# A graph layer that fetches source rows in three ways: gathers made to wait for ScalarE's copies, a new share for each way, and another order of the last octets

## The chip, the cores and the metric

One core of a Trainium2 chip runs the kernel. Its engines are TensorE (PE), VectorE (DVE), ScalarE (ACT), GpSimd (POOL) and SyncE (SP), each with an instruction stream of its own, and they wait for one another by semaphores. Times are microseconds (us) of device time for one execution. The profile is one execution seen by the hardware profiler: which engine did what, when, and what ended each wait. The clock that the profile lists is the share of full speed that TensorE was granted.

## The reference

A graph has 12,500 nodes with 64 features `x` and 400,000 edges, sorted by their destination `dst`; each edge has a source `src` and 16 attributes. One message-passing layer with a residual and a layer norm:

```
m_in = concat([x[src], x[dst], edge_attr], -1)
h = silu(m_in @ W1 + b1)
messages = silu(h @ W2 + b2)
agg = segment_sum(messages, dst, num_segments=12500)
y = silu(concat([x, agg], -1) @ W3 + b3)
out = layernorm(x + y, -1)
```

## The kernel before

**Tiles and octets.** 128 edges are a tile, and there are 3125 tiles. Eight tiles make an octet (`OT`), so that there are `NO` = 391 octets; the last has five tiles. Three octets make a chunk (`CT` = 24 tiles). The main loop runs over the octets by a counter `o`, which I call a turn, and its order on PE, ACT, DVE and SP is written out by hand (`tc.manual_schedule`); GpSimd's instructions go in the order in which they are issued.

**What an octet needs.** The first layer's input is summed in PSUM by TensorE (`first_layer`): the part of the source nodes, the part of the destination nodes (a window of `S` = 48 nodes, since `dst` is sorted) and the part of the attributes. ScalarE turns it into `h` (line 490). The second layer (`second_layer`) multiplies by W2, and ScalarE makes the messages `m` (line 505). `add_up` sums the messages of an octet by destination with one-hot matrices `eh`, and `add_window` (line 519, VectorE) adds the result at the window's place in `agg`. These steps belong to different turns: the second layer comes `SECOND` = 2 turns after the first, `add_up` `THIRD` = 4 and `add_window` `LAST` = 6, and the last few octets have shorter lags (`times`).

**Three ways to a source row.** The part of the source nodes comes

- by **gathers**: GpSimd issues an indirect DMA for each tile (`gather`, line 383), 128 rows of 64 numbers. In octets below `RAW` = 12 it reads `x`, from then on the table `pa` = x @ W1 (its first rows), which `table` builds in the first turns. The five buffers `ga` (`AHEAD` + 2) are filled three turns ahead; a buffer is free again when TensorE's first layer five octets earlier has read it.
- by **columns**: ScalarE and VectorE copy single columns of the transposed `x`, which lies in SBUF (`xs`), into a tile `cx` of 128 columns that holds two tiles of edges (`columns`, lines 307 and 309). The address of every column comes from a register; the registers are loaded from SBUF in groups (line 299). ScalarE makes `ACOLS` in two parts of 36, ahead of `h` and ahead of `m`; VectorE makes `VCOLS` in four parts, 68 in all. 256 copies replace two gathers of one octet; these octets are listed in `pairs`. The index list of each is loaded by SyncE (`index`) and turned into addresses by VectorE (`address`, line 368). Columns are made from octet `BEGIN` = 6 until `QUIET` = 6 octets ahead of the last.
- by **rows**: SyncE fetches single rows of `pa` by DMAs with a register as address (`rows`, line 336), `ROWS` = 16 a turn. 256 of them replace two gathers of one octet too; these octets are listed in `rpairs`.

An octet so has eight gathers, six, or four.

**Nodes.** Where all edges of a group of 512 nodes are done, the group's output follows (`node_load`, `node_product`, `node_silu`, `node_stats`, `divide`, `store`) in the turns set by `later`. The last two groups (`rest` and the one behind it) come after the loop.

**The check of dst.** Windows only work if every octet's destinations lie within 48 nodes and node groups aren't closed too early. `limits` computes this at the end on VectorE and `verdict` sums it over partitions with TensorE. If it fails, a second way (`general`) computes the layer again; with these inputs it does not run.

Of the kernel before, what the change touches and what calls it, by code (L numbers as in the profile page):

```python
# [9 lines left out]
F32 = mybir.dt.float32  # L10
# [10 lines left out]
P = 128  # L21
# [5 lines left out]
SCT = 240  # L27
AHEAD = 3
SECOND = 2
THIRD = 4  # L30
# [3 lines left out]
TABLES = 7  # L34
ACOLS = ((12, 12, 12), (12, 12, 12))
VCOLS = ((20,), (16,), (16,), (16,))
ROWS = 16
XADDR = 37088
QUIET = 6
LAG = CT * P // 32  # L40
# [62 lines left out]
def windows(ctx, tc, ident, identb, badi, pa, x, xt, xt2, src_c, src_row, dst_c, dst_row, attr_t, attr_2, base, w1, b1, w2, b2, w3, b3, out, edges):  # L103
# [154 lines left out]
    with tc.tile_pool(name="gat", bufs=AHEAD + 2) as gat, \  # L258
# [16 lines left out]
        while True:  # L275
# [3 lines left out]
            pairs.append(o)  # L279
        cols, indices = {}, {}  # L280
        xb = xs.bitcast(U8)

        def columns(o, eng, part):
# [5 lines left out]
            while cuts or left:  # L289
# [12 lines left out]
                for e, r in zip(range(e0, e0 + n), regs):  # L302
                    h = slice(e // P * D, (e // P + 1) * D)
                    to, frm = t[h, e % P * 4:e % P * 4 + 4], xb[:D, ds(r - XADDR, 4)]
                    if eng == ENG.DVE:

                        nc.vector.tensor_reduce(to, frm[:, :, None], AX.X, OP.max)  # L307
                    else:
                        nc.scalar.copy(to, frm)  # L309
                lo += n  # L310
# [11 lines left out]
        def rows(o):  # L322
            lo = (o - RAW) * ROWS
            j, e0 = lo // (2 * P), lo % (2 * P)
            if o < RAW or j >= len(rpairs):
                return
            if e0 == 0:
                single[rpairs[j]] = rx.tile([P, 2, D], F32, name="rx")
            t = single[rpairs[j]].bitcast(U8)
            if o % 2 == 0:  # L330
                _, rowreg[:] = nc.values_load_multi_w_load_instructions(
                    rindex[j][0:1, e0:e0 + 2 * ROWS], engines=(ENG.SP,), min_val=0, max_val=4 * D * (N - 1),
                    skip_runtime_bounds_check_because="src names a node")
            for e in range(e0, e0 + ROWS):
                r = rowreg.pop(0)
                nc.sync.dma_start(t[e % P:e % P + 1, e // P, :], pab[ds(r, 4 * D)].rearrange("(o n) -> o n", o=1))

        def rbegun(o):
            j = (o - RAW) * ROWS // (2 * P)
            return o >= RAW and (o - RAW) * ROWS % (2 * P) == 0 and j < len(rpairs), j  # L340

# [32 lines left out]
        def gather(o):  # L374
            c, t0, n, first, last = octs[o]
            ga = gat.tile([P, OT, D], F32, name="ga")
            sc = srcs[t0 // SCT][:, t0 % SCT:]
            if n % 2:
                nc.vector.memset(ga[:, n, :], 0.0)
            for i in range(n):  # L380
                if o in (pairs, rpairs)[i // 2 % 2] and i < 4:
                    continue
                nc.gpsimd.indirect_dma_start(  # L383
                    out=ga[:, i, :], out_offset=None, in_=x if o < RAW else pa[:, :],
                    in_offset=bass.IndirectOffsetOnAxis(ap=sc[:, i:i + 1], axis=0))
            got[o] = ga

# [215 lines left out]
        batches = [(q, min(q + RB, early - 1)) for q in range(0, early - 1, RB)]  # L603
        rest = early - 1
        for q in range(early):
            if q >= rest:
# [14 lines left out]
        def limits():  # L621
            evi = xs.bitcast(I32)[:, :3 * NCH]
            nc.gpsimd.iota(evi, pattern=[[STEP, NCH], [0, 3]], base=0, channel_multiplier=0)
            lag = xs[:, 3 * NCH:3 * NCH + NO]
            nc.vector.tensor_tensor(lag, evi[:, :NO], wb, op=OP.subtract)
            lim = nv.tile([P, 3], F32, name="lim")
# [22 lines left out]

        seconds = times({None: SECOND, 0: 1, 1: 1, 2: 1})  # L650
        adds = times({None: THIRD, 0: 2, 1: 2, 2: 2, 3: 3, 4: 3, 5: 3})
        folds = times({None: LAST, 0: 3, 1: 4, 2: 4, 3: 5})

        for o in range(min(AHEAD, NO)):
            gather(o)
# [14 lines left out]
        with tc.manual_schedule(engines={ENG.PE, ENG.Activation, ENG.DVE, ENG.SP}):  # L670
# [4 lines left out]
            for o in range(NO + 2):  # L675
# [31 lines left out]
                if o + 1 < NO - 1:  # L707
                    window_product(o + 1)
                if o % 4 == 0 and 4 <= o < NO + 4:
                    bases(ENG.DVE, o - 4)  # L710
                for q in folds.get(o, []):
# [27 lines left out]
                if 30 <= o < 30 + 2 * LP and o % 2 == 0:  # L739
                    k = (o - 30) // 2  # L740
                    part = rel[:, k * TILES // LP:(k + 1) * TILES // LP]
                    nc.vector.tensor_reduce(lims[:, 0, k:k + 1], part, AX.X, OP.min)
                    nc.vector.tensor_reduce(lims[:, 1, k:k + 1], part, AX.X, OP.max)
                if o >= 1:
                    for c in tables[(o - 1) * per:o * per]:
# [15 lines left out]
                if o == NO - 3:  # L761
                    node_product(rest, 1)
                if o == NO - 2:
                    for q in range(rest + 1, NG):
                        node_product(q, 1)


            for i in range(NO + 2, NO + LAST):
                for q in folds.get(i, []):
                    add_window(q)  # L770
            bad = limits()
            for q in behind.get(NO, []):
                node_silu(q)
            for f, a in todo.get(NO, []):
                f(*a)
            for q in range(rest, NG):
                node_product(q, 2)
                node_silu(q)
            for q in range(rest, NG):
                node_stats(q)  # L780
            verdict(bad)
            root(rest, NG)
# [261 lines left out]
```

## Time and profile before

| what | value |
|---|---|
| median of 3 runs | 5318.76 us (5303.48 to 5322.22) |
| the profiled execution | 5309.46 us |
| its span | 5307.7 us |
| mean granted TensorE clock | 0.644 |
| gathers, from `x` and from `pa` | 94 and 2575 |
| single rows fetched by SyncE | 5888 |
| column copies by ScalarE, by VectorE | 27000, 25480 |
| octets | 391 |

A group of the profile is read so: line, engine and operation, what it writes and reads, the count, busy time in all and the mean of one in ns, then the engine's idle time ahead of these instructions and what ended it. "issue" as the cause of idle time means that the engine waited for nothing that the profile can name. Copies overlap, so that 36 copies of 189 ns each take less than 36 times that. In a timeline the columns are start, length, engine, line, operation and count; in windows they are the stretch, its length, the busy time with the count in brackets, the granted clock, the share of DMA time and GB/s.

### The profile page before, as it was taken

The page shows a single profiled execution, that of the slowest core. Times are in us where ns is not written, and L with a number is a line of the kernel's source. Part 1 is how long each engine was busy: PE and PEld are TensorE (multiplying, and loading weights), DVE is VectorE, ACT ScalarE, POOL GpSimd, SP SyncE. Part 2 cuts the span into 40 slices and gives each one's busy share as a digit, 9 for nine tenths or more (in the row PEclk, how much of TensorE's full clock was granted, in tenths as well). Part 3 has the DMA queues.
Part 4 walks back from the last instruction along what each step waited for, and adds up shares of the span by engine and source line. Part 5 has one row for each costly group of instructions (what it writes and reads, how often), then busy time and mean ns, then how long its engine had stood idle before and what let it go on. Part 6 is the DMA issues. An engine that isn't in the chain of part 4 may idle for free. (4 is left out here: it accounts for less than half of the span.)

```text
span 5307.7 us, 110604 instructions
## 1 busy us (share of the span) xinstructions
PE 2676.8 (50%) x15336; PEld 1962.6 (37%) x15336; DVE 2676.6 (50%) x27690; ACT 3320.9 (63%) x27845; POOL 2520.4 (47%) x2678
## 2 busy tenths in 40 slices
PE   4644545444455455454554545544455455454555
PEld 3433333333333333333343333333333333333333
DVE  1555555545555555545555555555555555555552
ACT  1566666666666666666666666666666666666663
POOL 6444444444444444444444444444444444444443
PEclk6666666666666666666666666666666666666667
DMA  3111111111111111111111111111111111111111
GB/s 73 44 25 25 28 25 26 26 26 25 31 24 27 26 25 27 25 26 28 29 25 25 26 26 26 26 30 27 26 26 25 26 26 27 29 27 24 27 25 26
DMA packets 159906, 148.18 MB, mean 28 GB/s; under 512 B 103383, under 2 KB 111718, under 8 KB 158646
## 3 DMA queue, kind: packets, MB, share of 16 engines
q0 software_dynamic: 85408, 87.63, 8.7%
q1 hardware_dynamic: 59658, 45.35, 3.4%
q10 hardware_dynamic: 14092, 8.03, 0.6%
q14 instruction: 621, 5.09, 0.3%
q8 instruction: 127, 2.08, 0.2%
HBM read 134.37 MB, written 6.40 MB: 27 GB/s over the span
## 5 line engine op out<-in xcount | busy, mean ns | idle before, releaser
L309 ACT COPY cx<-xs 64x4 uint8 x27000 | 2879.8, 189 | 1568.0 <-issue 1534.5
L383 POOL DMA_INDIRECT ga<-pa,sc x2575 | 2429.3, 943 | 2679.8 <-PE p L483 1820.3
L307 DVE TENSOR_REDUCE cx<-xs 64x4 uint8 x25480 | 1946.1, 141 | 2076.7 <-issue 2045.6
L501 PEld LDWEIGHTS p<-w2d,h 128*128 128x128 f32 x3126 | 667.0, 315 | 2549.4 <-issue 2549.4
L499 PE MATMUL p<-b2r,one 3*128 3x512 bf16 x391 | 216.2, 553 | 2367.7 <-ACT m L505 1539.5
L501 PE MATMUL p<-w2d,h 128*128 128x128 f32 x3126 | 779.4, 427 | 3.0 <-issue 3.0
L487 PE MATMUL p<-oh,xw 128*128 128x512 f32 (+1 forms) x758 | 583.4, 865 | 0.9 <-issue 0.9
L514 PEld LDWEIGHTS pg<-eh,m 128*64 128x64 f32 x6250 | 248.5, 157 | 531.3 <-issue 266.5
L505 ACT ACTIVATE m<-p 128x512 f32<-128x512 f32 x391 | 231.8, 593 | 258.7 <-remote 164.7
L458 DVE COPY oh<-ph 96x512 f32<-96x512 f32 x391 | 266.1, 681 | 203.6 <-issue 193.0
L514 PE MATMUL pg<-eh,m 128*64 128x48 f32 x6250 | 299.4, 243 | 107.6 <-DVE agg L519 87.3
L483 PE MATMUL p<-ident,ga 128*128 128x128 f32 x1288 | 346.5, 411 | 1.3 <-issue 1.3
L490 ACT ACTIVATE h<-p 128x512 f32<-128x512 f32 x391 | 231.2, 591 | 76.7 <-remote 32.0
L483 PEld LDWEIGHTS p<-ident,ga 128*128 128x128 f32 x1288 | 276.1, 226 | 2.6 <-issue 2.6
L407 PE MATMUL mm<-w1bb,xr 65*96 65x128 f32 x782 | 265.5, 442 | 12.5 <-issue 5.4
L448 PE MATMUL ph<-identb,eh 128*96 128x128 bf16 x1563 | 245.2, 311 | 51.5 <-remote 21.6
L448 PEld LDWEIGHTS <-eh 128*96 128x96 bf16 x1563 | 233.0, 198 | 62.3 <-DVE oh L458 26.9
L430 DVE TENSOR_TENSOR eh<-wrow,dc 128x384 f32<-128x384 f32 x392 | 213.3, 544 | 10.5 <-remote 10.0
L487 PEld LDWEIGHTS p<-oh,xw 128*128 128x128 f32 x758 | 190.6, 308 | 0.9 <-issue 0.9
L407 PEld LDWEIGHTS mm<-w1bb,xr 65*96 65x96 f32 x782 | 170.7, 277 | 14.8 <-issue 10.0
L412 DVE TENSOR_TENSOR xw<-mm,mask 96x128 f32<-96x128 f32 x391 | 110.1, 281 | 125.4 <-issue 78.5
L486 PE MATMUL p<-cx,w1d 128*128 128x128 f32 x408 | 122.0, 399 | 0.0
(89 smaller groups left out, 945.5 us busy)
## 6 DMA issues: line engine op xcount, KB each, us to landing
rx<-pa SPq DMA_DIRECT2D x5888, 0.2 KB
ga<-pa,sc POOLq DMA_INDIRECT x2575
oh<-in_attr SPq DMA_DIRECT2D x130, 192.0 KB
xr<-in_xt SPq DMA_DIRECT2D x391, 24.0 KB
cxi<-in_src_row SPq DMA_DIRECT2D x205, 1.0 KB
xs<-in_xt ACTq DMA_DIRECT2D x6, 512.0 KB
pa<-v ACTq DMA_DIRECT2D x12, 256.0 KB
xa<-in_x SPq DMA_DIRECT2D x24, 128.0 KB
```

Of the source, the lines that this page charges most:

```text
L307: nc.vector.tensor_reduce(to, frm[:, :, None], AX.X, OP.max)
L309: nc.scalar.copy(to, frm)
L383: nc.gpsimd.indirect_dma_start(out=ga[:, i, :], out_offset=None, in_=x if o < RAW else pa[:, :], in_offset=bass.IndirectOffsetOnAxis(ap=sc ...
L407: nc.tensor.matmul(pw[:E, :], winrow[o], w1bb.rearrange("k s m -> k (s m)"), start=True, stop=True)
L448: nc.tensor.matmul(ph[:E, i, :], eh[:, i, :, 1], identb, start=(i == 0), stop=(i == k - 1), skip_group_check=True)
L458: nc.vector.tensor_copy(oh[:E, :], ph[:E, :(n + 1) // 2].rearrange("p i e -> p (i e)"))
L483: nc.tensor.matmul(p1[:, i, :], g2.rearrange("p s d -> p (s d)"), ident, is_transpose=True, start=(i == c), stop=False, skip_group_check=True)
L487: nc.tensor.matmul(p1[:, :k], xw[o % 3], oh, start=False, stop=True, skip_group_check=True)
L490: nc.scalar.activation(h[:, :k], p1[:, :k], AF.Silu)
L501: nc.tensor.matmul(p2[:, 2 * i:2 * i + 2, :].rearrange("p s d -> p (s d)"), h[:, i, :], w2d, start=False, stop=(i == k - 1), skip_group_ch ...
L505: nc.scalar.activation(m[:, :n2], p2[:, :n2], AF.Silu)
L514: nc.tensor.matmul(pg[s * D:(s + 1) * D, :], m[:, i, :], eh[:, i // 2, :, s], start=(i < 2), stop=(i >= n - 2), skip_group_check=True)
```

## The change

- **Waits.** Every column copy is noted in `steps` under the turn that makes it. A gather of octet `o` now also waits, by a dependency added by hand, for one of ScalarE's copies: with `LEAD` = 4 it is a copy of turn `o` - 4, and gather k of n waits for the copy that stands k/n of the way through that turn's list. Where there are no more copies than gathers there is no wait, as in the first turns.
- **Shares.** ScalarE makes 36 + 38 columns a turn instead of 36 + 36, VectorE 70 instead of 68, SyncE fetches 18 rows instead of 16. `rows`, `rbegun` and with them `rload` and `raddress` are written so that a list of 256 may begin within a turn. `QUIET` falls from 6 to 2.
- **The last octets.** The lags of the last eight octets are shortened: second layer 0 or 1 turns behind the first, `add_up` 1 or 2, `add_window` 2 or 3.
- **The last node groups.** Of the two groups behind the loop, the first is multiplied, put through silu and its statistics taken in the last two turns of the loop; only the last group stays behind it.
- **The check.** `limits` is cut in two. Its iota is issued ahead of the first gather and has 131 numbers instead of 393; the rest, `check`, runs in turn 51 (31 + 2 `LP`), `verdict` in turn 52.
- **Bases.** VectorE loads the window bases of four octets in turns 2, 6, 10 and so on, for octets from `o` - 2, instead of in turns 4, 8, 12 for octets from `o` - 4.

```diff
+LEAD = 4
+TURNS = (ENG.Activation,)
...
-ACOLS = ((12, 12, 12), (12, 12, 12))
-VCOLS = ((20,), (16,), (16,), (16,))
-ROWS = 16
+ACOLS = ((12, 12, 12), (12, 12, 14))
+VCOLS = ((20,), (16,), (18,), (16,))
+ROWS = 18
 XADDR = 37088
-QUIET = 6
+QUIET = 2
...
+        steps = {ENG.Activation: {}, ENG.DVE: {}}
...
-                        nc.vector.tensor_reduce(to, frm[:, :, None], AX.X, OP.max)
+                        done = nc.vector.tensor_reduce(to, frm[:, :, None], AX.X, OP.max)
                     else:
-                        nc.scalar.copy(to, frm)
+                        done = nc.scalar.copy(to, frm)
+                    steps[eng].setdefault(o - (eng == ENG.Activation and part == 0), []).append(done.ins)
...
         def rows(o):
-            lo = (o - RAW) * ROWS
-            j, e0 = lo // (2 * P), lo % (2 * P)
-            if o < RAW or j >= len(rpairs):
-                return
-            if e0 == 0:
-                single[rpairs[j]] = rx.tile([P, 2, D], F32, name="rx")
-            t = single[rpairs[j]].bitcast(U8)
-            if o % 2 == 0:
-                _, rowreg[:] = nc.values_load_multi_w_load_instructions(
-                    rindex[j][0:1, e0:e0 + 2 * ROWS], engines=(ENG.SP,), min_val=0, max_val=4 * D * (N - 1),
-                    skip_runtime_bounds_check_because="src names a node")
-            for e in range(e0, e0 + ROWS):
+            for lo in range((o - RAW) * ROWS, (o + 1 - RAW) * ROWS) if o >= RAW else ():
+                j, e = lo // (2 * P), lo % (2 * P)
+                if j >= len(rpairs):
+                    return
+                if e == 0:
+                    single[rpairs[j]] = rx.tile([P, 2, D], F32, name="rx")
+                if e % 32 == 0:
+                    _, rowreg[:] = nc.values_load_multi_w_load_instructions(
+                        rindex[j][0:1, e:e + 32], engines=(ENG.SP,), min_val=0, max_val=4 * D * (N - 1),
+                        skip_runtime_bounds_check_because="src names a node")
+                t = single[rpairs[j]].bitcast(U8)
                 r = rowreg.pop(0)
                 nc.sync.dma_start(t[e % P:e % P + 1, e // P, :], pab[ds(r, 4 * D)].rearrange("(o n) -> o n", o=1))
 
         def rbegun(o):
-            j = (o - RAW) * ROWS // (2 * P)
-            return o >= RAW and (o - RAW) * ROWS % (2 * P) == 0 and j < len(rpairs), j
+            j = -(-(o - RAW) * ROWS // (2 * P))
+            return o >= RAW and j * 2 * P < (o + 1 - RAW) * ROWS and j < len(rpairs), j
 
...
-            for i in range(n):
-                if o in (pairs, rpairs)[i // 2 % 2] and i < 4:
-                    continue
-                nc.gpsimd.indirect_dma_start(
+            todo = [i for i in range(n) if o not in (pairs, rpairs)[i // 2 % 2] or i >= 4]
+            for k, i in enumerate(todo):
+                g = nc.gpsimd.indirect_dma_start(
                     out=ga[:, i, :], out_offset=None, in_=x if o < RAW else pa[:, :],
                     in_offset=bass.IndirectOffsetOnAxis(ap=sc[:, i:i + 1], axis=0))
+                eng = TURNS[k % len(TURNS)]
+                ahead = steps[eng].get(o - LEAD - (eng == ENG.Activation), [])
+                if len(ahead) > len(todo):
+                    tc.add_manual_dep(g.ins, ahead[k * len(ahead) // len(todo)].name,
+                                      mybir.DependencyInfo(mybir.DependencyClass.Sync, mybir.DependencyReason.DATA))
...
         def limits():
-            evi = xs.bitcast(I32)[:, :3 * NCH]
-            nc.gpsimd.iota(evi, pattern=[[STEP, NCH], [0, 3]], base=0, channel_multiplier=0)
-            lag = xs[:, 3 * NCH:3 * NCH + NO]
-            nc.vector.tensor_tensor(lag, evi[:, :NO], wb, op=OP.subtract)
+            evi = nv.tile([P, NCH], I32, name="evi")
+            nc.gpsimd.iota(evi, pattern=[[STEP, NCH]], base=0, channel_multiplier=0)
+            return evi
+
+        def check(evi):
+            lag = nv.tile([P, NO], F32, name="lag")
+            f, k = NO // 3, NO // 3 * 3
+            nc.vector.tensor_tensor(lag[:, :k].rearrange("p (c t) -> p c t", t=3), evi[:, :f, None].to_broadcast([P, f, 3]),
+                                    wb[:, :k].rearrange("p (c t) -> p c t", t=3), op=OP.subtract)
+            if k < NO:
+                nc.vector.tensor_tensor(lag[:, k:], evi[:, f:f + 1].to_broadcast([P, NO - k]), wb[:, k:], op=OP.subtract)
...
-        seconds = times({None: SECOND, 0: 1, 1: 1, 2: 1})
-        adds = times({None: THIRD, 0: 2, 1: 2, 2: 2, 3: 3, 4: 3, 5: 3})
-        folds = times({None: LAST, 0: 3, 1: 4, 2: 4, 3: 5})
-
+        seconds = times({None: SECOND, 0: 0, 1: 0, **{k: 1 for k in range(2, 8)}})
+        adds = times({None: THIRD, 0: 1, 1: 1, **{k: 2 for k in range(2, 8)}})
+        folds = times({None: LAST, 0: 2, 1: 2, **{k: 3 for k in range(2, 8)}})
+
+        evi = limits()
...
-                if o % 4 == 0 and 4 <= o < NO + 4:
-                    bases(ENG.DVE, o - 4)
+                if o % 4 == 2 and o - 2 < NO:
+                    bases(ENG.DVE, o - 2)
...
+                if o == 31 + 2 * LP:
+                    bad = check(evi)
+                if o == 32 + 2 * LP:
+                    verdict(bad)
...
-                    node_product(rest, 1)
+                    node_product(rest + 1, 1)
                 if o == NO - 2:
-                    for q in range(rest + 1, NG):
-                        node_product(q, 1)
+                    node_product(rest)
+                    node_silu(rest)
+                if o == NO - 1:
+                    node_stats(rest)
 
 
             for i in range(NO + 2, NO + LAST):
                 for q in folds.get(i, []):
                     add_window(q)
-            bad = limits()
             for q in behind.get(NO, []):
                 node_silu(q)
             for f, a in todo.get(NO, []):
                 f(*a)
-            for q in range(rest, NG):
-                node_product(q, 2)
-                node_silu(q)
-            for q in range(rest, NG):
-                node_stats(q)
-            verdict(bad)
+            node_product(rest + 1, 2)
+            node_silu(rest + 1)
+            node_stats(rest + 1)
```

## What I expected

> **What bounds the kernel now.** I read the page first: busy times, then the costliest groups.
>
> ```profile
> PE 2676.8 (50%) x15336; PEld 1962.6 (37%) x15336; DVE 2676.6 (50%) x27690; ACT 3320.9 (63%) x27845; POOL 2520.4 (47%) x2678
> ...
> L309 ACT COPY cx<-xs 64x4 uint8 x27000 | 2879.8, 189 | 1568.0 <-issue 1534.5
> L383 POOL DMA_INDIRECT ga<-pa,sc x2575 | 2429.3, 943 | 2679.8 <-PE p L483 1820.3
> L307 DVE TENSOR_REDUCE cx<-xs 64x4 uint8 x25480 | 1946.1, 141 | 2076.7 <-issue 2045.6
> ```
>
> No engine is full. ScalarE is the fullest, and its 1568.0 us of idle time ahead of the column copies are nearly all "issue": it waited for nothing that the profile names. VectorE shows the same ahead of its own column copies. The waits by engine tell how such idle time is cut up:
>
> ```profile
> DVE cx L307 <- issue: 2045.6, 3031, 6.2
> ACT cx L309 <- issue: 1534.5, 2161, 5.5
> ```
>
> ScalarE has 2161 gaps of 1534.5/2161 = 0.71 us, VectorE 3031 of 0.67 us. GpSimd's idle time ahead of gathers is put down to TensorE's first layer (1820.3 us above): it issues an octet's gathers in one run and then waits for a buffer. To see whether the two belong together I read the timeline of two neighbouring octets, GpSimd and then ScalarE:
>
> ```profile
> 2022.08 0.94 POOL L383 DMA_INDIRECT ga<-pa,sc  x1 [8.85 <-PE p L483]
> ...
> 2030.82 0.94 POOL L383 DMA_INDIRECT ga<-pa,sc  x1 [0.30 <-issue]
> 2034.05 0.94 POOL L383 DMA_INDIRECT ga<-pa,sc  x1 [2.28 <-PE p L487]
> ...
> 2040.28 0.94 POOL L383 DMA_INDIRECT ga<-pa,sc  x1 [0.30 <-issue]
> ```
>
> ```profile
> 2016.82 0.60 ACT L505 ACTIVATE m<-p 128x512 f32<-128x512 f32 x1
> 2017.31 3.62 ACT L309 COPY cx<-xs 64x4 uint8 x36
> 2020.96 0.60 ACT L490 ACTIVATE h<-p 128x512 f32<-128x512 f32 x1
> 2021.45 3.52 ACT L309 COPY cx<-xs 64x4 uint8 x36
> 2024.88 0.58 ACT L505 ACTIVATE m<-p 128x512 f32<-128x512 f32 x1
> ...
> 2044.22 0.60 ACT L505 ACTIVATE m<-p 128x512 f32<-128x512 f32 x1
> ```
>
> One run has eight gathers, (2030.82 - 2022.08)/7 = 1.25 us apart, the next six. From one m to the next, ScalarE needs 8.06 us for the first octet (72 copies at 3.52/36 = 0.098 us, h and m) and 19.34 us for the second, which has the same work. Their mean, 13.70, is the kernel's mean octet, 5307.7/391 = 13.57. The same stretch in windows, with line 309's copies alone (length, busy time, count, clock):
>
> ```profile
> 2017.30:2021.00 3.70, 3.61 (x36) 0.50 0.00 1
> 2022.08:2025.85 3.77, 3.24 (x34) 0.95 0.14 29
> 2025.87:2033.36 7.49, 1.85 (x12) 0.56 0.13 27
> 2033.36:2037.38 4.02, 3.43 (x34) 0.82 0.25 65
> 2037.38:2042.57 5.19, 1.25 (x8) 0.50 0.17 31
> 2042.57:2048.40 5.83, 5.17 (x52) 0.50 0.01 2
> ```
>
> This is what bounds the kernel. For the first 3.3 to 3.8 us of a run of gathers ScalarE copies as fast as without any; then it makes 12 copies in 7.49 us and 8 in 5.19, and is fast again at 2033.36 and 2042.57. The slow stretch ends 11.28 us after the first of eight gathers (2022.08) and 8.52 after the first of six (2034.05), so at 1.38n + 0.24: it behaves like a backlog worked off at 1.38 us a gather, while GpSimd adds one every 1.25. After a pause of 2034.05 - 2033.36 = 0.7 us the next run had its full fast start again. The clock column doesn't go with it (0.56 and 0.50 slow, 0.50 and 0.95 fast).
>
> The Trainium skill speaks against all this: "SBUF — State Buffer", section "Who interferes with whom", says that DMA never contends with a compute engine and that "PE and ACT never wait on anyone". By it, moving gathers would give ScalarE nothing. The windows disagree (36 copies in 3.70 us against 12 in 7.49, one engine and line); what the rule would make of the time is the second rival.
>
> **The change part by part.**
>
> *The waits.* Gather k of n of octet X now waits for copy 74k/n that ScalarE makes in loop turn X-4. The old wait for the buffer (first layer of X-5) is met by then, as h of X-5 stands ahead of those copies. Behind a waiting gather stand only later gathers; TensorE waits for them in turn X, three turns after the last release, at least 24 us at 8.06 a turn. So lateness is covered; without that cover a 1.25 us gather would delay the first layer one for one. Released by copies 0, 12, 24, 37, 49, 61 (n = 6) the gathers form groups of three, cut by h and m; with n = 8, groups of four. 12 copies take 1.2 us and 9 take 0.9, both under 1.25, so within a group GpSimd sets the pace; but a slow ScalarE, at about 0.63 us a copy (7.49/12, 5.19/8), releases the next only after 5 to 8 us, so a run cannot grow through a slow stretch as it does now.
>
> A run of n costs the slow stretch less its copies: 12 x 0.098 of 7.49 and 8 x 0.098 of 5.19, so 85% of 1.38n + 0.24 - b, where b, the start, is 3.3 to 3.8. With b = 3.3 that is 6.8 us for eight, 4.4 for six, 2.1 for four, 0.9 for three. From octet 12 to 386 the loops give 160, 203 and 12 octets of eight, six and four gathers before, and 156, 201 and 18 after. Before: (160 x 6.8 + 203 x 4.4 + 12 x 2.1)/375 = 5.4 us an octet, and 8.06 + 5.4 = 13.5, near the 13.57 above. After, in two groups each: (156 x 4.2 + 201 x 1.8)/375 = 2.7. Saved: 2.7 at b = 3.3; with b = 3.8, 4.9 - 1.9 = 3.0. Runs of three and four are drawn down from the rows of six and eight. The bounds: groups of three may not reach the slow stretch at all, or groups may join across h, which lasts 0.6 us. I take off 0.1 for the second.
>
> *74, 70 and 18.* ScalarE: 2 x 0.098 = 0.2 us an octet, on the path. VectorE's two cost its group's (1946.1 + 2045.6)/25480 = 0.157 us each at most, 0.3, under ScalarE's 8.26; were that cover gone, they would add 0.3. SyncE's row transfers have a row of their own:
>
> ```profile
> 2016.89 2.46 SPq L336 DMA_DIRECT2D rx<-pa  x8
> ```
>
> 2 x 2.46/8 = 0.6 us more; 18 rows are 5.5 us, also within the octet. There are 213 column pairs for 205 and 26 row pairs for 23, hence 22 gathers fewer (2647), already in the counts above.
>
> ```profile
> L368 DVE TENSOR_SCALAR cxi<-cxi 1x256 int32<-1x256 int32 x205 | 56.2, 274 | 1.1
> ```
>
> Their index lists are eleven more (those of the rows cost about the same): 11 x 0.274 = 3 us of VectorE, under ScalarE; uncovered, 3 us.
>
> *The end.* Columns now reach the last octets, and gathers stay paced there. Before, a long run stands there:
>
> ```profile
> 5232.92 0.98 POOL L383 DMA_INDIRECT ga<-pa,sc  x1 [0.86 <-PE pg L514]
> ...
> 5251.68 0.94 POOL L383 DMA_INDIRECT ga<-pa,sc  x1 [0.30 <-issue]
> ...
> 5253.76 0.82 PEld L514 LDWEIGHTS pg<-eh,m 128*64 128x64 f32 x13 [9.79 <-issue]
> ...
> 5291.58 0.56 DVE L625 TENSOR_TENSOR xs<-xs,wb 128x391 f32<-128x391 int32 x1
> 5291.71 3.17 PE L554 MATMUL mm<-w3s,agg 128*128 128x64 f32 x16 [0.53 <-DVE agg L519]
> ```
>
> Sixteen gathers in a row, in which even TensorE stands 9.79 us. Cutting that run is worth about 10; the second last node group taken out of the final chain saves half of the 3.17 us of matmuls and its statistics, about 3; shorter lags 2. I take 15 in all, between 0 and 30. *The check of dst* leaves the end, where its first 0.56 us operation and those after it overlap the 3.17 us of matmuls, so that is worth nothing; in octet 51 it costs VectorE under 2 us once. The iota goes ahead of the first gather, which waits for its indices anyhow (below), and is a third as large:
>
> ```profile
> 2.84 1.11 POOL L383 DMA_INDIRECT ga<-in_x,sc  x1 [1.35 <-DMA sc<-in_src_c]
> ...
> 5230.83 1.23 POOL L623 IOTA xs<- 128x393 int32 x1
> ```
>
> The bases for VectorE are loaded two turns sooner, as many as before: nothing, or one register load of an octet if they hold up the queue.
>
> *The sum.* Per octet 2.8 (the middle of 2.7 and 3.0) - 0.1 - 0.2 = 2.5 us; 375 x 2.5 = 940; with the end 955. The profiled execution took 5309.5 us, 1.8 more than its span and 9 less than the median of the runs, which is within their spread. 5309.5 - 955 = 4350, rounded. For this case alone the gain lies between 1.8 and 3.3 us an octet: 4060 to 4620.
>
> **The rivals.**
>
> *No slow stretch is left.* Each wait may stretch GpSimd's step past 1.38 us, and the backlog never forms. Then 6.74 gathers an octet x 1.38 = 9.3 us bind, more than ScalarE's 8.26: 5309.5 - 375 x 4.3 - 15 = 3680. For it: in neither run did the first 3.3 us slow anything. Against: 1.2 us between releases, and POOL's step of 1.25.
>
> *ScalarE's gaps are its own.* If the slow copies have nothing to do with gathers, a copy costs (2879.8 + 1534.5)/27000 = 0.163 us, and 213 x 256 x 74/144 = 28,021 copies are 1021 more: +167, less 15 for the end, 5460. This is what the skill's rule in that section would give. Against it stand the six windows.
>
> *Every gather drags its own slow 1.38 us once they are spread (the slower side).* If the fast start of a run does not come back between spaced gathers, 6.74 x 1.38 x 0.85 = 7.9 us an octet are lost instead of 5.4: 375 x (2.5 + 0.2) more, 6320. It decides from the point where the mean gather costs more than 5.4/6.79 = 0.8 us. Against it: 0.7 us of pause brought the fast start back; for it: pauses inside a group will be shorter.
>
> *Runs of eight stay.* 8 x 1.25 = 10 us exceed an octet of 8.26, so GpSimd may fall behind and go on without waits. Octets of eight would keep 6.8: (156 x 6.8 + 201 x 1.8)/375 = 3.8, a gain of 1.4 an octet: 4770.
>
> **How the numbers follow.** Forecast 0.60, no slow stretch 0.16, runs of eight 0.11, gaps of its own 0.06, every gather 0.05, a gain under 0.5% for reasons not seen 0.02 (half a per cent is about what this measurement tells from none). Faster 0.87, same 0.02, slower 0.11. The range, 3650 to 4900, takes in the forecast, the first and the last rival; the rest is 0.13 and some of their far ends.
>
> **What would show it.** Right: "issue" gaps ahead of ScalarE's copies fall from 1534.5 to near half; GpSimd's idle time ahead of gathers is put down to ScalarE's copies instead of TensorE's first layer; runs of three and four with slow windows under 3 us; octets near 11 us without the change between 8 and 19. Wrong: slow windows while gathers start over 1.4 us apart; runs still of six and eight; TensorE waiting for gathers.

## The result, and the profile after

| | before | after |
|---|---|---|
| time, median | 5318.73 us (5303.48 to 5322.22) | 6395.67 us (6389.73 to 6396.54) |
| ratio to before, 95% interval | 1 | 1.2029 (1.2005 to 1.2053) |
| span of the profiled execution | 5307.7 us | 6394.7 us |
| mean octet, span / 391 | 13.57 us | 16.35 us |

The changed kernel is 20% slower; 4350 us was forecast. The page of the changed kernel, busy times and the rows that answer to those of before (the gathers are now line 385, ScalarE's copies 312, VectorE's 310):

```profile
PE 2972.5 (46%) x15344; PEld 2040.3 (32%) x15344; DVE 2577.8 (40%) x28704; ACT 3338.9 (52%) x28891; POOL 2500.9 (39%) x2656
...
L385 POOL DMA_INDIRECT ga<-pa,sc x2553 | 2410.6, 944 | 3762.9 <-ACT cx L312 3165.4
L310 DVE TENSOR_REDUCE cx<-xs 64x4 uint8 x26482 | 1839.1, 140 | 3626.2 <-issue 3457.4
L312 ACT COPY cx<-xs 64x4 uint8 x28046 | 2832.5, 188 | 447.7 <-issue 428.6
```

Two signs that the prediction named for "right" are there, the first more strongly than named: ScalarE's issue gaps ahead of its copies fell from 1534.5 to 428.6 us, and GpSimd now waits for ScalarE's copies. The octet near 11 us is not. And VectorE's issue gaps ahead of its own copies rose from 2045.6 to 3457.4. The waits of the changed kernel (us in total, times, longest) show who is late because of it:

```profile
DVE cx L310 <- issue: 3457.4, 1532, 4.3
POOL ga L385 <- ACT cx L312: 3196.1, 963, 16.0
ACT h L497 <- PE p L494: 1775.2, 353, 7.7
PEld L455 <- DVE oh L465: 1684.4, 257, 8.9
```

Before, VectorE had 3031 gaps of 0.67 us; now it has half as many, 1532, of 2.26 us. TensorE waits for VectorE's oh, and ScalarE for TensorE's first layer: ScalarE's own gaps went down and its wait for h (76.7 us in all before) went up. VectorE's timeline in the changed kernel over one octet, with the idle time ahead of each row in brackets:

```profile
2005.13 0.54 DVE L437 TENSOR_TENSOR eh<-wrow,dc 128x384 f32<-128x384 f32 x1
2009.23 1.36 DVE L310 TENSOR_REDUCE cx<-xs 64x4 uint8 x20 [3.56 <-issue]
2010.52 0.27 DVE L419 TENSOR_TENSOR xw<-mm,mask 96x128 f32<-96x128 f32 x1
2013.99 1.21 DVE L310 TENSOR_REDUCE cx<-xs 64x4 uint8 x16 [3.20 <-issue]
2015.21 0.69 DVE L465 COPY oh<-ph 96x512 f32<-96x512 f32 x1
2018.66 1.23 DVE L310 TENSOR_REDUCE cx<-xs 64x4 uint8 x18 [2.77 <-issue]
2020.40 1.10 DVE L310 TENSOR_REDUCE cx<-xs 64x4 uint8 x16 [0.50 <-issue]
```

Three of VectorE's four groups of copies stand behind some 3 us of nothing, the fourth behind 0.50. "Issue" hides a real instruction here. Register instructions aren't counted as busy, and the instruction ahead of each group is a load of as many registers (line 302, the addresses of the columns). The single records of the trace have its duration, for the same stretch:

```
start us   ns     instruction
2004.65   4497    TENSOR_LOAD  VectorE line 302, 20 registers, place 74
2009.92   3612    TENSOR_LOAD  VectorE line 302, 16 registers, place 94
2014.53   4048    TENSOR_LOAD  VectorE line 302, 18 registers, place 110
2019.21   1103    TENSOR_LOAD  VectorE line 302, 16 registers, place 128
```

The first three take 0.225 us a register (4.50/20, 3.61/16, 4.05/18), the fourth 0.069. All of VectorE's loads in the trace sum to 1783 us before and to 4913 us after, and by the single records 3463 of VectorE's 3627 us of idle time ahead of its copies lie inside such loads now, against 577 of 2078 before. Before, 16 registers took 1.10 us and 20 took 1.35, wherever they stood. "Place" is where a group begins in the list of the octet's columns, worked out from ACOLS and VCOLS: before, VectorE's groups began at 72, 92, 108 and 124, all multiples of four; 74 columns for ScalarE put three of the four two past one. One octet's loads are now 4.50 + 3.61 + 4.05 + 1.10 = 13.3 us, and from the first of them to the next octet's first (2021.13) go 16.5 us, about the mean octet of 16.35.

**Theory A**, from this: the change is slow because 74 and 18 move VectorE's groups off multiples of four; the waits do what was forecast. **Theory B**, the rival: the waits themselves make it slow, since GpSimd now follows ScalarE's copies, which follow TensorE, which follows the gathers, and spaced gathers each bring their slow time along (the prediction's rival at 6320 us).

### The profile page after: what moved, and what is told of

Read it like the earlier page. It is cut to its first block, busy times and chain, and to the rows that moved or that the text cites. A ratio compares the mean times of both kernels' runs of the same rounds, so it can differ in the third digit from the quotient of the medians.

```text
span 6394.7 us, 116460 instructions
## 1 busy us (share of the span) xinstructions
PE 2972.5 (46%) x15344; PEld 2040.3 (32%) x15344; DVE 2577.8 (40%) x28704; ACT 3338.9 (52%) x28891; POOL 2500.9 (39%) x2656
## 5 line engine op out<-in xcount | busy, mean ns | idle before, releaser
L310 DVE TENSOR_REDUCE cx<-xs 64x4 uint8 x26482 | 1839.1, 140 | 3626.2 <-issue 3457.4
L312 ACT COPY cx<-xs 64x4 uint8 x28046 | 2832.5, 188 | 447.7 <-issue 428.6
L455 PEld LDWEIGHTS <-eh 128*96 128x96 bf16 x1563 | 176.5, 187 | 2523.7 <-DVE oh L465 1684.4
L521 PE MATMUL pg<-eh,m 128*64 128x48 f32 x6250 | 374.5, 282 | 883.5 <-DVE agg L526 576.8
L521 PEld LDWEIGHTS pg<-eh,m 128*64 128x64 f32 x6250 | 316.1, 194 | 1432.0 <-DVE agg L526 953.6
L494 PE MATMUL p<-oh,xw 128*128 128x512 f32 (+1 forms) x758 | 706.2, 1035 | 0.0
L494 PEld LDWEIGHTS p<-oh,xw 128*128 128x128 f32 x758 | 206.4, 332 | 0.0
L385 POOL DMA_INDIRECT ga<-in_x,sc x94 | 89.2, 949 | 82.5 <-ACT cx L312 30.7
```

The lines of the kernel that those rows point to most:

```text
L310: done = nc.vector.tensor_reduce(to, frm[:, :, None], AX.X, OP.max)
L312: done = nc.scalar.copy(to, frm)
L385: g = nc.gpsimd.indirect_dma_start(out=ga[:, i, :], out_offset=None, in_=x if o < RAW else pa[:, :], in_offset=bass.IndirectOffsetOnAxis(a ...
L455: nc.tensor.matmul(ph[:E, i, :], eh[:, i, :, 1], identb, start=(i == 0), stop=(i == k - 1), skip_group_check=True)
L494: nc.tensor.matmul(p1[:, :k], xw[o % 3], oh, start=False, stop=True, skip_group_check=True)
L521: nc.tensor.matmul(pg[s * D:(s + 1) * D, :], m[:, i, :], eh[:, i // 2, :, s], start=(i < 2), stop=(i >= n - 2), skip_group_check=True)
```

## The experiments

Each run stands beside runs of the kernel before on the same chip. The chips differ, as the last part shows, so ratios count here, not times.

### Undoing one part: e1_fours, e2_before_74_66, e3_no_waits, e4_before_waits

On this chip the kernel before took 5404.01 us.

**e1_fours**: the change, with groups on multiples of four.

```diff
-ACOLS = ((12, 12, 12), (12, 12, 14))
-VCOLS = ((20,), (16,), (18,), (16,))
+ACOLS = ((12, 12, 12), (12, 12, 12))
+VCOLS = ((20,), (16,), (20,), (16,))
```

> The change with its waits, its 18 rows and its end, but ScalarE's groups all of 12 (72 columns) and VectorE's of 20, 16, 20 and 16 (72), so that as many columns and gathers are left as in the change, and every group begins on a multiple of four and has a multiple of four registers. Theory A (VectorE's register loads cost 0.225 us a register instead of 0.068 where a group begins off a multiple of four): VectorE's load gaps fall back, and the octet is what the prediction gave, 11 us: 4350 us, between 4000 and 4700. Theory B (the waits themselves make the kernel slow): nothing changes that matters, 6300 to 6450 us.

Measured: 4511.72 us, 0.834 of before (0.8322 to 0.8358). Two numbers changed in the lists, and 20% slower turns into 17% faster. Its rows:

```profile
L385 POOL DMA_INDIRECT ga<-pa,sc x2553 | 2409.1, 944 | 1888.8 <-ACT cx L312 1248.5
L312 ACT COPY cx<-xs 64x4 uint8 x27288 | 2860.1, 189 | 778.4 <-issue 740.1
L310 DVE TENSOR_REDUCE cx<-xs 64x4 uint8 x27240 | 1978.5, 141 | 1170.0 <-issue 1115.2
```

VectorE's gaps fall to a third of 3457.4, with 758 more copies. Theory A holds, B falls: the waits are all in this kernel.

**e2_before_74_66**: the kernel before, with three groups off the fours and no wait.

```diff
-ACOLS = ((12, 12, 12), (12, 12, 12))
-VCOLS = ((20,), (16,), (16,), (16,))
+ACOLS = ((12, 12, 12), (12, 12, 14))
+VCOLS = ((20,), (16,), (14,), (16,))
```

> The kernel before, without any wait, with 74 columns for ScalarE (last group 14) and 66 for VectorE (20, 16, 14, 16): as many columns in all, but three of VectorE's groups begin two past a multiple of four. Theory A: VectorE stands some 3 us ahead of each of these three groups and the octet comes near 16 us: 5900 to 6400 us. Theory B: no wait, no loss: 5250 to 5450 us.

Measured: 6255.64 us, 1.1572 (1.1549 to 1.1596). Two columns moved, and the groups moved with them, make the old kernel slow without any wait. Its rows:

```profile
L309 ACT COPY cx<-xs 64x4 uint8 x27750 | 2944.1, 190 | 1546.6 <-issue 1526.4
L307 DVE TENSOR_REDUCE cx<-xs 64x4 uint8 x24730 | 1762.5, 141 | 3430.6 <-issue 3412.6
```

**e3_no_waits**: the changed kernel without the dependency.

```diff
-                if len(ahead) > len(todo):
+                if False:
```

> The changed kernel with the waits on ScalarE's copies left out and all else kept. Theory A: VectorE's loads stay slow and ScalarE's slow stretches come back beside them: 6350 us or more, up to 7300. Theory B: near the time before, 5250 to 5450 us.

Measured: 6787.21 us, 1.2556 (1.2531 to 1.2581). Even in the slow kernel the waits are a gain: 1.2556 without them, 1.2029 with them (on another chip, where the kernel before took 5318.73 us). ScalarE and VectorE in it:

```profile
L312 ACT COPY cx<-xs 64x4 uint8 x28046 | 2979.1, 189 | 1510.5 <-issue 1493.6
L310 DVE TENSOR_REDUCE cx<-xs 64x4 uint8 x26482 | 1871.4, 141 | 3568.9 <-issue 3555.3
```

**e4_before_waits**: the kernel before with LEAD, TURNS, `steps` and the dependency alone; 72, 68 and 16 as before.

> The kernel before with the waits alone (gathers wait for ScalarE's copies of four octets back), columns 72 and 68, 16 rows, and the end as before. Theory A: the whole of what the prediction gave for the waits, octet 10.8 to 11.6 us: 4250 to 4550 us. Theory B: 6200 to 6400 us.

Measured: 4528.76 us, 0.8375 (0.8361 to 0.8389). ScalarE's waits in it:

```profile
POOL ga L386 <- ACT cx L312: 1257.9, 1097, 13.5
...
ACT cx L312 <- issue: 716.6, 1479, 3.6
```

So the waits by themselves halve ScalarE's gaps (716.6 of 1534.5) and would take, by this ratio, 0.1625 x 5318.7 = 864 us off the time of the first runs.

### What makes a load slow: e5_counts

Its edit, against e1_fours:

```diff
-VCOLS = ((20,), (16,), (20,), (16,))
+VCOLS = ((20,), (18,), (18,), (16,))
```

> As e1_fours, but VectorE's groups are 20, 18, 18 and 16: the first 18 begins on a multiple of four (92), the second two past one (110). Theory A1 (the place where a group begins decides): the load of the first 18 takes 16 x 0.068 + 2 x 0.225 = 1.5 us, that of the second 18 x 0.225 = 4.05, loads 8.0 us an octet in place of 4.9, and the time rises little above e1_fours', as VectorE comes just up to ScalarE: 4550 to 5000 us. Theory A2 (a count that is no multiple of four decides): both take 4.05, loads 10.6 us an octet, some 5200 to 5500 us.

Measured: 4938.67 us, 0.9296 (0.9258 to 0.9334; before 5316.50 here). VectorE's single loads in the trace: 1.35 us for 20 at place 72, 1.57 to 1.59 for the 18 at place 92, 4.06 for the 18 at place 110, 1.10 for 16 at 128. Theory A1 came out nearly to the number: it gave 16 x 0.068 + 2 x 0.225 = 1.54 and 18 x 0.225 = 4.05. What decides is where a group begins; a group that begins on four pays the dear price only for what is left over beyond whole fours. In the timeline of this kernel the 18 behind the slow load:

```profile
2015.10 1.36 DVE L310 TENSOR_REDUCE cx<-xs 64x4 uint8 x20 [0.84 <-issue]
...
2023.96 1.23 DVE L310 TENSOR_REDUCE cx<-xs 64x4 uint8 x18 [3.04 <-issue]
2025.70 1.11 DVE L310 TENSOR_REDUCE cx<-xs 64x4 uint8 x16 [0.51 <-issue]
```

It is a dose as well: loads of 4.9, 8.0 and 13.3 us an octet give ratios of 0.834, 0.930 and 1.203.

### What the rest of the change is worth: e6_fours_no_waits, e8_68_76

**e6_fours_no_waits** is e1_fours with e3_no_waits' edit.

> As e1_fours, without the waits: what is left of the change then are 22 gathers fewer, 72 columns for VectorE, 18 rows and the new end. If the waits made e1_fours fast: near the kernel before, 5300 to 5450 us, with ScalarE's gaps back at 1500 us. If the fours, fewer gathers or the end made it fast: near 4500 us.

Measured: 5361.15 us, 1.0087 (1.0062 to 1.0112), ScalarE's issue gaps 1533.8 us. Fewer gathers, 18 rows and the new end together are no gain at all without the waits.

**e8_68_76** moves four columns of e1_fours from ScalarE to VectorE, on fours; its edit against e1_fours:

```diff
-ACOLS = ((12, 12, 12), (12, 12, 12))
-VCOLS = ((20,), (16,), (20,), (16,))
+ACOLS = ((12, 12, 12), (12, 12, 8))
+VCOLS = ((20,), (20,), (20,), (16,))
```

> As e1_fours, with 68 columns for ScalarE (last group 8) and 76 for VectorE (20, 20, 20, 16), every group on a multiple of four. Theory (ScalarE's copies set the octet once the loads are right, 0.098 us each as in the prediction): 378 x 4 x 0.098 = 150 us less than e1_fours, 4360 us. Rival (the gathers and their waits or VectorE set it): 4500 us or more.

Measured: 4567.94 us, 0.8598 (0.8577 to 0.862), slower than e1_fours, where 150 us less were expected. With 76 columns VectorE ends last: TensorE's wait for VectorE's oh, too small in e1_fours to be among its longest waits, is 789.7 us here. ScalarE's 0.098 us a copy isn't the price of an octet by itself; VectorE stands close behind.

### Does pacing alone end the slow stretch: e7_pace, e9_pace_small, e10_pace_wide

These are e6_fours_no_waits, so without waits, and GpSimd gets a memset to do between gathers, of 128x256 numbers in e7_pace and e10_pace_wide and of 128x128 in e9_pace_small.

```diff
+                for p in fill:
+                    tc.add_manual_dep(g.ins, p.ins.name, order)
+                fill[:] = [nc.gpsimd.memset(pace, 0.0)]
+                tc.add_manual_dep(fill[0].ins, g.ins.name, order)
```

e7_pace has the memset without the three lines that hold it in its place.

> As e6_fours_no_waits, with one GpSimd memset of 128x256 after each gather (a 128x128 one took 0.205 us in the trace of before and after, so 0.3 is assumed), so that gathers start some 1.55 us apart and wait for no copy. Theory of the backlog (a gather is worked off in 1.38 us, and only a run that is issued faster than that slows ScalarE): hardly any slow stretch is left, 6.6 x 1.55 = 10.2 us an octet bind: 3950 to 4300 us. Rival (a run of more than three in a row is slow, however it is spaced up to some 0.7 us of pause): slow stretches stay as long as before or grow: 5300 us or more.

Measured: 6094.01 us, 1.1469 (1.1441 to 1.1497). It isn't the test it was meant to be: the memsets stand in bundles, most of them of 70 to 80, with runs of gathers in between, the gathers of a run are still 1.25 us apart, and the time goes where TensorE waits for late gathers (917.0 us, longest 25.8).

> As e6_fours_no_waits, with one memset of 128x128 (0.205 us) now held by the order of the program between each two gathers, so that they start some 1.25 + 0.205 + 0.06 = 1.5 us apart, with no wait for a copy. (In e7_pace the memsets had been put in bundles ahead of the runs, and gathers inside a run stayed 1.25 us apart.) Theory of the backlog (1.38 us a gather): nearly no slow stretch, the gathers' pace of 6.6 x 1.5 = 9.9 us sets the octet: 3850 to 4150 us. Rival (a run of more than three is slow however it is spaced): 5350 us or more.

> The same with memsets of 128x256 (0.312 us in e7_pace), gathers some 1.62 us apart. Backlog: no slow stretch either, 6.6 x 1.62 = 10.7 us an octet, 4150 to 4350 us, slower than e9_pace_small by about 0.1 us a gather. Rival: 5350 us or more; if the backlog's true pace lies between 1.5 and 1.62, this one is the faster of the two.

Measured: 5248.57 us, 0.9885 (0.9868 to 0.9901), and 4958.06 us, 0.9332 (0.9314 to 0.9351). Part of each memset fits into the 0.30 us between two gathers, so that starts came 1.3 to 1.4 us apart in the one and 1.45 in the other. GpSimd in e10_pace_wide, and ScalarE beside it:

```profile
2012.14 0.95 POOL L388 DMA_INDIRECT ga<-pa,sc  x1 [5.21 <-PE p L497]
2013.10 0.33 POOL L393 MEMSET pace<- 128x256 f32 x1
2013.59 0.95 POOL L388 DMA_INDIRECT ga<-pa,sc  x1 [0.17 <-issue]
...
2019.37 0.95 POOL L388 DMA_INDIRECT ga<-pa,sc  x1 [0.17 <-issue]
```

```profile
2011.75 2.75 ACT L315 COPY cx<-xs 64x4 uint8 x28
2015.78 0.86 ACT L315 COPY cx<-xs 64x4 uint8 x8 [1.28 <-issue]
2018.00 0.60 ACT L519 ACTIVATE m<-p 128x512 f32<-128x512 f32 x1 [1.36 <-ACT cx L315]
2018.50 1.24 ACT L315 COPY cx<-xs 64x4 uint8 x11
2020.20 0.38 ACT L315 COPY cx<-xs 64x4 uint8 x3 [0.47 <-issue]
```

The stretch begins 2.4 us after the first gather (3.3 to 3.8 in the first profile), though these six come (2019.37 - 2012.14)/5 = 1.45 us apart, slower than the 1.38 at which the backlog was to be worked off. It is only looser: ScalarE's issue gaps are 1095.8 us in all, against 1533.8 in e6_fours_no_waits. So the backlog's rule (slow only where gathers come faster than 1.38 us) is wrong; slow windows with starts over 1.4 us apart were one of the prediction's signs of being wrong. Waits on ScalarE's copies, with their longer pauses, leave 740.1 and do better than even spacing.

### Where the slow stretch is missing: e11 to e18

**e11_fixed_address**, again as **e13_fixed_again** and **e17_fixed_third**: the kernel before, in which VectorE copies from one fixed address and so loads no registers. It leaves out the fetching itself: VectorE's columns all hold the first node's numbers, and the output is not the layer's.

```diff
-                        nc.vector.tensor_reduce(to, frm[:, :, None], AX.X, OP.max)
+                        nc.vector.tensor_reduce(to, xb[:D, 0:4][:, :, None], AX.X, OP.max)
```

> The kernel before, but VectorE loads no registers and copies all of its columns from one fixed address (so its columns hold the first node's, and the load of 4.7 us an octet is gone); ScalarE's loads and copies, the gathers and the rows are as before. Theory F1 (the gathers slow ScalarE's copies by themselves): ScalarE keeps its issue gaps of some 1500 us ahead of copies, and the time stays near the kernel before, 5100 to 5350 us. Theory F2 (it takes VectorE's register copies beside ScalarE's; in the changed kernel, where VectorE mostly stands loading, runs of three and four hardly slow ScalarE): the gaps fall below 700 us and the time to 4000 to 4500 us.

> The kernel of e11_fixed_address once more (VectorE copies its columns from one fixed address and loads no registers), since the chip of that run showed no slow stretch for the kernel before either. On a chip where the kernel before takes some 5300 us: theory F1 (gathers slow ScalarE's register copies by themselves): ScalarE's issue gaps stay near 1500 us, 5100 to 5350 us; theory F2 (VectorE's register copies are needed too): gaps under 700 us, 4000 to 4500 us. Where the kernel before takes 3374 us: 3374 again, and nothing told.

> The kernel of e11_fixed_address again. Where the kernel before takes some 5300 us: theory F1 (gathers slow ScalarE's register copies by themselves) 5100 to 5350 us, with ScalarE's issue gaps near 1500; theory F2 (VectorE's register copies are needed too) 4000 to 4500 us, gaps under 700. Where the kernel before takes some 3370: the same, and nothing told.

Measured: 3374.07, 3374.70 and 3373.63 us. But the kernel before, on the same chips, took 3374.45, 3370.93 and 3372.86 us: 1.0002 (0.9992 to 1.0012), 1.0011 (1.0000 to 1.0022) and 1.0004 (0.9993 to 1.0014). There was no slow stretch to take away, and F1 and F2 aren't told apart. ScalarE and GpSimd in e11_fixed_address:

```profile
L309 ACT COPY cx<-xs 64x4 uint8 x27000 | 2668.9, 190 | 27.2 <-issue 10.1 <-DMA pa<-v 2.2
L383 POOL DMA_INDIRECT ga<-pa,sc x2575 | 2434.3, 945 | 785.2 <-issue 683.6 <-DMA ga<-pa,sc 68.0 <-PE p L501 8.8
```

As many copies and as many gathers as in the first profile, at 945 ns a gather (943 there), but 10.1 us of gaps in place of 1534.5, with gathers in unbroken runs.

**e12_76_68** and **e14_76_68_again** are e1_fours with ((12, 12, 12), (12, 12, 16)) and ((20,), (16,), (16,), (16,)).

> As e1_fours, with 76 columns for ScalarE (last group 16) and 68 for VectorE (20, 16, 16, 16), every group on a multiple of four: twice the change's own shift towards ScalarE, without the slow loads. If ScalarE's 0.098 us a copy lie on the path: 378 x 4 x 0.098 = 148 us more than e1_fours, 0.86 of before. If VectorE has become the one that ends last (as e8_68_76 came out slower with four more columns for it): less than e1_fours, 0.81 to 0.83 of before.

> The kernel of e12_76_68 once more. On a chip where the kernel before takes some 5300 us: if ScalarE's copies lie on the path, 148 us more than e16_fours_again beside it; if VectorE ends last, less than that one. On a chip like that of e12_76_68: 1.02 of before again.

**e15_change** is the changed kernel, **e16_fours_again** is e1_fours.

> The changed kernel itself. Theory A gives VectorE's loads the same price on any chip: 6000 to 6400 us whether the kernel before takes 5300 us here or 3374. If the price of a load goes with the slow stretch: 3400 to 3800 us on a chip like that of e12_76_68.

> The kernel of e1_fours once more. On a chip where the kernel before takes some 5300 us: 0.83 to 0.84 of it. On a chip without the slow stretch the waits can save nothing: 3350 to 3450 us, 0.99 to 1.02.

Measured: e12_76_68 1.0216 (1.0199 to 1.0233), e14_76_68_again 1.026 (1.023 to 1.029). Beside the latter, e15_change 6319.46 us, 1.874 (1.8685 to 1.8794), and e16_fours_again 3387.43 us, 1.0045 (1.0034 to 1.0056). VectorE in e15_change and ScalarE's timeline in e16_fours_again:

```profile
L310 DVE TENSOR_REDUCE cx<-xs 64x4 uint8 x26482 | 1835.4, 140 | 3621.8 <-issue 3421.1 <-ACT cx L312 118.0 <-ACT m L512 72.3
```

```profile
2003.48 0.60 ACT L512 ACTIVATE m<-p 128x512 f32<-128x512 f32 x1
2004.11 3.52 ACT L312 COPY cx<-xs 64x4 uint8 x36
2007.65 0.60 ACT L497 ACTIVATE h<-p 128x512 f32<-128x512 f32 x1
2008.14 3.65 ACT L312 COPY cx<-xs 64x4 uint8 x36
2011.70 0.59 ACT L512 ACTIVATE m<-p 128x512 f32<-128x512 f32 x1
```

The loads cost the same on either kind of chip (VectorE's sum to 4913 us in both traces of the changed kernel; its gaps are 3421.1 us here and 3457.4 in the first). The waits save nothing where there is nothing to save, and cost 0.45% with the rest of the change. From m to m go 8.22 us: the prediction's octet without a stretch, 8.06, all the time. Four copies more for ScalarE (e14_76_68_again against e16_fours_again) are 72 us, half of 378 x 4 x 0.098 = 148.

**e18_before_68_72**: the kernel before, four columns moved to VectorE, on fours, no wait.

```diff
-ACOLS = ((12, 12, 12), (12, 12, 12))
-VCOLS = ((20,), (16,), (16,), (16,))
+ACOLS = ((12, 12, 12), (12, 12, 8))
+VCOLS = ((20,), (16,), (20,), (16,))
```

> The kernel before without any wait, ScalarE's last group 8 in place of 12 (68 columns) and VectorE's third 20 in place of 16 (72), 140 in all as before, every group on a multiple of four. On a chip where the kernel before takes some 3370 us: if ScalarE's copies set the octet, 4 x 0.098 us x 391 = 150 us less, 3220; if VectorE comes up to it, 3300 or more. Where it takes some 5300: the runs of gathers go on unbroken, 0.97 to 1.01 of it.

Measured: 3375.51 us, 1.0014 (1.0004 to 1.0024). No gain: TensorE's wait for VectorE's oh is 592.6 us here. On these chips no version tried beats the kernel before; on the others e1_fours beats both kernels.

## Why the prediction was wrong

**The failed step** is in the part on 74, 70 and 18: "VectorE's two cost its group's (1946.1 + 2045.6)/25480 = 0.157 us each at most, 0.3, under ScalarE's 8.26". The mean of a group of rows was taken as the price of one column more. But 577 us of the idle time in it lie inside register loads, and the price of a load hangs on where its group begins, which 74 moves for three of VectorE's four groups and not for two columns. In place of 0.3 us, VectorE's loads grew by 13.3 - 4.7 = 8.6 us an octet, and VectorE came to set the octet. The rows to see it were not in the grouped views; the loads stood in the trace of before (1.10 us for 16, 1.35 for 20), all on fours, so that no row of before had the dear price. The step should have asked what "issue" ahead of VectorE's copies was made of before it put a bound on it; that price, unseen in the trace, was not bounded from above.

The Trainium skill, "Runtime: NRT & Kernel Launch", section "Instruction fetch mechanics", gives some 200 ns a register for a TENSOR_LOAD even in bulk; the page speaks of loads from HBM, while these come from SBUF. The runs come near that figure off the fours (225 ns) and are far below it on them (68 ns). An estimate by that page's figure, 0.2 us for each of 70 registers, makes VectorE's loads 14 us an octet, near the 13.3 measured after and far from the 4.7 before.

**The waits** gave nearly what was forecast, on the chips that have the slow stretch. ScalarE's gaps halved (716.6 us in e4_before_waits), GpSimd's idle time went over to ScalarE's copies, the octet was 4529.7/391 = 11.6 us where "near 11" was said. Their term was 2.7 us an octet; measured 864/375 = 2.3. Not all of the working behind it holds: the runs came out shorter than the threes and fours that were forecast (in e4_before_waits 277 gathers stand alone, and there are 470 runs of two, 239 of three and 132 of four, counting starts less than 1.5 us apart), and the pace of 1.38 us falls with e10_pace_wide. With groups on fours, as in e1_fours, 0.834 x 5318.7 = 4436 us (4426 to 4445) would be the time, within the forecast's own 4060 to 4620.

**ScalarE's two copies** were to cost 0.2 us an octet. Its load of 14 took 1.23 us in place of 0.78 for 12, which is 2 x 0.225; neither lies on the path in the changed kernel, where ScalarE waits for h.

**The end and the small edits**, 15 us forecast: from the start of the last m to the end of the span there were 17.6 us before and 13.5 in e1_fours, so the final chain did shrink, by 4.1 us, where 3 were named for the node group taken out of it:

```profile
5290.09 0.49 ACT L505 ACTIVATE m<-p 128x384 f32<-128x384 f32 x1 [1.95 <-PE p L501]
```

```profile
4502.66 0.49 ACT L512 ACTIVATE m<-p 128x384 f32<-128x384 f32 x1 [3.46 <-PE p L508]
```

But as a whole these edits, with 72 and 72 columns, are a loss of 0.9% without the waits (e6_fours_no_waits); with them e1_fours is 17 us faster than e4_before_waits. SyncE's two more rows and the check of dst were not run alone.

**The rivals.** "Every gather drags its own slow time" named 6320 us, close to the result, by a mechanism that is not the one at work: e1_fours spaces the gathers as the change does and is fast. "No slow stretch is left" rested on the rule that gathers more than 1.38 us apart form no backlog; e10_pace_wide shows that they still do. "ScalarE's gaps are its own" falls on the chips with the slow stretch, where spacing the gathers and nothing else halved the gaps (e4_before_waits). On the two chips of e11 to e18, where unbroken runs of gathers leave ScalarE 10.1 us of gaps, the waits gave nothing (e16_fours_again). The rule of the Trainium skill that stands behind that rival ("SBUF — State Buffer", section "Who interferes with whom") fits these two chips and not the others. "Runs of eight stay" did not come: e4_before_waits has four of them, the kernel before 162.

**What stays open.** Why ScalarE has the slow stretch on some chips and not on others; the kernels, the gathers' 0.94 us and their 1.25 us from start to start are the same. The same kernel was traced on both kinds as e1_fours and e16_fours_again, the kernel before only on the slow kind. In the runs here the short time came each time with the fixed-address kernel run on the same chip, on two chips in three rounds of runs; whether that is chance wasn't tried. The slow stretch is not ScalarE's alone: in the first profile 1438 of the 2757 copies of ScalarE that start over 0.5 us after the one before them start within 0.05 us of such a copy of VectorE, against 41 of 749 in e18_before_68_72, so that the two engines seem to be held and let go together; by what, no run shows.

What e11_fixed_address was to tell, whether ScalarE's slow stretch needs VectorE's copies beside it (F2) or not (F1), is in part told by two other runs. In e2_before_74_66 and e3_no_waits VectorE stands in its dear loads as in the changed kernel, and ScalarE still has 1526.4 and 1493.6 us of gaps; of 1417 us between neighbouring copies of ScalarE in e2_before_74_66, 913 fall where VectorE stands in a load of over 2.9 us and copies nothing. That speaks for F1: the copies of VectorE are not needed, though its loads may play a part. So VectorE's standing does not by itself explain why the changed kernel has only 428.6 us of gaps and e1_fours, with the same waits, 740.1. In e15_change, without a slow stretch, ScalarE has 318.9 us of them too, so that little of the 428.6 is left for the slow stretch. Why so little stays open: the same gathers are spread over octets of 16.35 us there, but no run changed that alone.

## What to carry to other kernels

Before a boundary between engines moves, ask what sits at the boundary: a count of 74 in place of 72 cost ScalarE 0.65 us at most and VectorE 8.6, because three of VectorE's four groups behind it began off a multiple of four. "Issue" ahead of a group is not free time of unknown kind; look up the uncounted instructions in it (register loads above all) one by one, before a mean over the group is used as a price. And run the kernel before beside every experiment on the same chip: what a change is worth went from 0.834 to 1.0045 between chips with one and the same kernel.

## What the runs showed of the hardware

- A load of registers took 0.068 us a register in fours that begin on a multiple of four, 0.225 us for each register otherwise (on VectorE 18 registers took 1.57 us at place 92 and 4.06 at place 110). On ScalarE, whose groups all began on fours, 12 took 0.78 us and 14 took 1.23.
- The same kernel took 5296 to 5410 us on some chips and 3368 to 3376 on others; whether it is the chip or something else in those runs isn't shown. The kernel of e1_fours, traced on both kinds, has spans of 4516.2 and 3377.9 us with gathers of 944 and 945 ns and ScalarE's copies of 189 and 190; the gaps ahead of ScalarE's copies are 740.1 and 13.2 us, those ahead of VectorE's 1115.2 and 559.2.
- Where the slow stretch exists, it began 2.4 to 3.8 us after the first gather of a run in the timelines read, also with gathers 1.45 us apart. ScalarE's gaps were 1533.8 us with unbroken runs, 1095.8 with gathers 1.45 us apart and 740.1 with waits on copies.
